# Pacing woven stages by an account of three engines and their buffers

## The chip, the cores and the metric

The kernel runs on one core of one Trainium2 chip. The metric is the time of one execution on the device in microseconds (us); a lower time is better. Before the change the median of the first three runs was 7,900.34 us (7,895.84 to 7,903.62).

The engines are called by their names or as the profile has them: VectorE (DVE), ScalarE (ACT), TensorE (PE; PEld is its weight load), GpSimd (POOL), and SyncE (SP), which starts the transfers (1,321 in the built program; three more are started by ScalarE).

## The reference, cut to what matters

Sixteen images of 32 channels, 128 x 128, pass through four layers. Each layer normalises its input in groups of channels and adds its own result to the input.

```python
x = x + L0(gn(x))   # a row LSTM
x = x + L1(gn(x))   # quantise, then out[f] = -sum over 32 channels and 9 taps of |patch - w[f]|
x = x + L2(gn(x))   # Hartley transform to 32 x 32 modes, mix the channels, transform back
x = x + L3(gn(x))   # five edge operators, normalised; conv1 160 -> 32; a small encoder and decoder
return x
```

Layer 1 fixes the shape of the program. A sum of absolute differences is no matrix product: the differences have to be made elementwise, and only their sum over channels is a product with a matrix of ones.

## The kernel before

Layer 0 fills the first 935 us. Then comes a loop over 16 images x 2 halves x 72 taps, 2,304 in all. One tap makes one tile of 128 x 8,192 differences, on VectorE (`d_dve`, three buffers) or on ScalarE (`d_act`, two buffers), and 16 matmuls on TensorE sum it into four tiles of 128 x 512 in PSUM (called banks here), where the matmuls of this kernel put their results. Taking a result out of PSUM is called an eviction here. A tile's buffer comes free when its sum is done: of the 512 us that VectorE idles before its taps, 476 end with a sum, and 878 of 931 on ScalarE. Between the taps, groups of four images of layers 2 and 3 are woven in as a Python generator. It emits instructions and yields what they cost: a positive number is TensorE time, a negative one is time to wait before going on. The class `Weave` decides after each tap how far the generator may go. The order in which Python emits instructions is the order in each engine's queue, because `keep_order` pins it. The trace of this kernel, set beside the built program by line and tile, keeps to it: ScalarE starts all of its 3,126 instructions in that order, VectorE all but 16 of 7,177, and no matmul starts more than 0.85 us ahead of one that stands before it. So everything below is about the order in which queues are filled; no arithmetic depends on it.

```python
class Weave:
    def advance(self, pe):
        us = (self.dve + self.act) / 2 - self.now      # one clock, the mean of two engines
        self.now += us
        self.credit = min(self.credit + us - pe, 4.0)   # TensorE time that is left over
        self.hold = max(self.hold - us, 0.0)
        self.due(self.now)                              # run the steps put off until now
        if self.credit < 1.0:
            return
        while self.credit > 0 and not self.hold and self.step():
            pass

DVE_US, ACT_US, PE_US = 2.28, 7.1, 0.87

class Differences:
    def run(self, tc, ctx, weave):
        ...
        for i in range(72):
            if i == 3:
                ...                      # new banks, the linear part, the sums of taps 0 to 2
            ...
            act = weave.act + ACT_US < weave.dve + DVE_US and 3 <= i < 68 and len(late) < 2
            t = dp.tile([128, R, P], F16, name="d_act" if act else "d_dve", bufs=2 if act else 3)
            ...
            if act:
                nc.scalar.activation(dst, src, AF.Relu, bias=self.neg[:, i : i + 1])
                weave.act += ACT_US
                late.append((acc, t, i))
            else:
                nc.vector.tensor_scalar(dst, src, self.qw[:, i : i + 1], 0.0, ALU.subtract, ALU.max)
                weave.dve += DVE_US
                while late and (i - late[0][2] > 4 or i == 71):
                    self.sums(*late.pop(0))          # a ScalarE tile: more than 4 taps later
                ...
                self.sums(acc, t, i)                 # a VectorE tile: at once
            weave.advance(4.0 * PE_US + 4.0 if i == 3 else PE_US)
```

What is not yet emitted when the last tap is done (the end of the third group of images and the whole fourth) is emitted by `drain`, and that is the tail of the program.

Of the kernel before, what the change touches and what calls it, by code (L numbers as in the profile page):

```python
# [292 lines left out]
class Weave:  # L293
# [7 lines left out]

    def __init__(self, work):
        self.work, self.pending = work, None
        self.now = self.base = self.credit = self.hold = self.dve = self.act = 0.0
        self.finished, self.count, self.put_off = -1, 0, []
# [6 lines left out]

    def done(self, v):

        if v in self.put_off:
            self.put_off.remove(v)
            v[2]()

    def due(self, now):

        while self.put_off and min(self.put_off)[0] <= now:
            v = min(self.put_off)
            self.put_off.remove(v)
            self.base = v[0]
            v[2]()
        self.base = self.now

    def step(self):

        v = self.pending or next(self.work, None)  # L330
        self.pending = None
        if v is None:
            return False
        if isinstance(v, tuple):
            if v[1] > self.finished:
                self.pending = v
                return False
        elif v < 0:
            self.hold = -v
        else:  # L340
            self.credit -= v
            self.spent = v
        return True

    def advance(self, pe):


        us = (self.dve + self.act) / 2 - self.now
        self.now += us
        self.credit = min(self.credit + us - pe, 4.0)  # L350
        self.hold = max(self.hold - us, 0.0)
        self.due(self.now)
        if self.credit < 1.0:
            return
        while self.credit > 0 and not self.hold and self.step():
            pass


def drain(*weaves):

    live = list(weaves)
    while live:
        w = min(live, key=lambda w: w.now)
        w.spent = 0.0
        go = w.step()
        w.now += w.spent + w.hold
        w.hold = 0.0
        w.due(w.now if go else float("inf"))
        if not go:
# [18 lines left out]
DVE_US, ACT_US, PE_US = 2.28, 7.1, 0.87  # L388


def rest(nc, tc, cst, sel16, bias, m1, r1, a, d, out):


    with ExitStack() as ctx:
# [15 lines left out]
        end.weave.now, end.weave.finished = weave.now, B - 1  # L410
# [3 lines left out]
class Differences:  # L414
# [100 lines left out]
    def finish(self, b, half, acc, xr):  # L515
# [12 lines left out]
        self.weave.later(6.0, store)  # L528
        self.weave.dve += 5.6

    def sums(self, acc, d, i):
        c = 1 if i % 3 == 1 else 0
        for k in range(4):
            for j in range(4):
# [6 lines left out]
                    stop=i == 71,  # L541
# [18 lines left out]
    def run(self, tc, ctx, weave):  # L560
# [12 lines left out]
        before, following = None, self.loaded(0, 0)  # L573
        for b in range(B):
            for half in range(2):
                q = following
                late, ahead, xq = [], [], {}
                for i in range(72):
                    if i == 3:
# [3 lines left out]
                        weave.advance(0.0)  # L583
                        acc = [ps.tile([128, 512], F32, name="acc1") for _ in range(4)]
                        self.linear(acc, q)
                        for t, n in ahead:
                            self.sums(acc, t, n)
# [4 lines left out]
                    if half == 0 and b + 1 < B:  # L592
# [6 lines left out]
                        k = (i - 22) // 15  # L599
                        if 0 <= k < 4 and (i - 22) % 15 == 0:  # L600
# [3 lines left out]
                    act = weave.act + ACT_US < weave.dve + DVE_US and 3 <= i < 68 and len(late) < 2  # L604
# [3 lines left out]
                    dst = t if kw == 1 else t[:, :, :W]  # L608
                    if act:
                        nc.scalar.activation(dst, src, AF.Relu, bias=self.neg[:, i : i + 1])  # L610
                        weave.act += ACT_US
                        late.append((acc, t, i))
                    else:
                        nc.vector.tensor_scalar(dst, src, self.qw[:, i : i + 1], 0.0, ALU.subtract, ALU.max)  # L614
                        weave.dve += DVE_US
                        while late and (i - late[0][2] > 4 or i == 71):
                            self.sums(*late.pop(0))
                        if i < 3:
                            ahead.append((t, i))
                            weave.advance(0.0)  # L620
                            continue
                        self.sums(acc, t, i)
                    weave.advance(4.0 * PE_US + 4.0 if i == 3 else PE_US)
# [5 lines left out]
def normalised(nc, pool, ps, weave, mv, n, avg, eps, out):  # L629
# [6 lines left out]
    yield -4.5  # L636
# [8 lines left out]
    yield -4.5  # L645
# [1171 lines left out]
```

## Time and profile before

| stretch of the profiled execution | us | idle of VectorE | idle of ScalarE |
|---|---|---|---|
| front: layer 0 | 934.7 | | |
| woven: taps of layer 1 with layers 2 and 3 between | 5,707.2 | 913 | 991 |
| tail: what layers 2 and 3 have left | 1,242.8 | | |
| span | 7,884.7 | | |

Idle is the length of the stretch less the engine's busy time in it. The prediction shows the profile's lines for these numbers. A line of waits names who waited for whom, then the total in us, the number of waits and the longest one.

```profile
PE acc L536 <- DVE d_dve L614: 838.8, 567, 28.6
PE acc L536 <- ACT d_act L610: 494.7, 211, 16.4
```

TensorE stands 839 us for VectorE tiles and 495 us for ScalarE tiles.

### The profile page before, as it was taken

What the parts mean: (1) busy time and instruction counts of PE and PEld (TensorE: products, weight loads), DVE (VectorE), ACT (ScalarE), POOL (GpSimd) and SP (SyncE); (2) the same over time, 40 slices, a digit from 0 to 9 for tenths busy, and PEclk for the clock granted to TensorE, in tenths of its full rate; (3) what the DMA queues carried; (4) which work ended last, traced back from release to release, by engine and by line L of the source; (5) the groups of instructions that cost most, each with busy time, mean ns of one, the idle gap of its engine ahead of it and who ended that gap; (6) DMA issues with size and microseconds to landing.
All of it is one profiled execution on the core that took longest, in us unless ns stands there. A gap on an engine that the chain in (4) does not pass through costs nothing. (4 is left out here: it accounts for less than half of the span.)

```text
span 7884.7 us, 258419 instructions
## 1 busy us (share of the span) xinstructions
PE 5635.8 (71%) x121132; PEld 3165.4 (40%) x121132; DVE 5847.9 (74%) x7177; ACT 5406.7 (69%) x3129; POOL 21.6 (0%) x15
## 2 busy tenths in 40 slices
PE   3788366566677668886676666897667765997797
PEld 3665222222253334442343343343335333555564
DVE  7787599989969797887877978888787877134213
ACT  2565488799869879887778877887887885123122
POOL 0000000000000000000000000000000000000000
PEclk9899788888878779998868788998787887897896
DMA  8653111111132431112332432120333233434314
GB/s 319 223 181 130 59 50 60 48 52 39 50 116 80 123 102 51 58 33 67 79 98 90 129 89 73 40 70 34 88 86 101 87 102 94 116 107 122 91 33 90
DMA packets 374269, 721.68 MB, mean 92 GB/s; under 512 B 50896, under 2 KB 219856, under 8 KB 362320
## 3 DMA queue, kind: packets, MB, share of 16 engines
q1 hardware_dynamic: 372768, 704.58, 29.4%
q8 instruction: 949, 15.55, 0.8%
q14 instruction: 120, 0.98, 0.0%
q10 hardware_dynamic: 432, 0.57, 0.0%
HBM read 507.21 MB, written 164.32 MB: 85 GB/s over the span
## 5 line engine op out<-in xcount | busy, mean ns | idle before, releaser
L610 ACT ACTIVATE d_act<-q,neg 128x8192 f16<-128x8192 f16 (+1 forms) x612 | 4332.5, 7137 | 930.9 <-PE acc L536 877.6
L614 DVE TENSOR_SCALAR d_dve<-q,qw 128x8192 f16<-128x8192 f16 (+1 forms) x1692 | 3906.2, 2361 | 512.0 <-PE acc L536 476.3
L536 PE MATMUL acc<-d_dve,sel 128*32 128x512 f16 x27072 | 2007.5, 432 | 861.6 <-DVE d_dve L614 838.8
L536 PEld LDWEIGHTS <-sel 128*32 128x32 f16 x36864 | 1121.1, 106 | 2800.6 <-issue 2196.8
L536 PE MATMUL acc<-d_act,sel 128*32 128x512 f16 x9792 | 784.5, 446 | 499.1 <-ACT d_act L610 494.7
L1519 PE MATMUL acc<-xp,wf 32*32 32x512 f32 x25600 | 986.0, 625 | 29.0 <-issue 16.1
L1519 PEld LDWEIGHTS acc<-xp,wf 32*32 32x32 f32 x25600 | 478.8, 105 | 378.1 <-issue 244.6
L1458 ACT ACTIVATE y<-pooled,b 32x128 f32<-32x128 f32 x512 | 204.6, 400 | 532.2 <-DVE pooled L1444 525.1
L223 PE MATMUL pg<-h,wb 64*64 64x20 f32 (+15 forms) x4096 | 401.2, 323 | 102.4 <-DVE h L255 67.0
L753 PE MATMUL acc<-y,u_conv 32*32 32x256 f32 (+1 forms) x9728 | 402.2, 511 | 79.3 <-issue 35.8
L223 PE MATMUL pg<-e,wb 64*64 64x20 f32 (+15 forms) x4096 | 353.2, 318 | 24.7 <-DVE e L258 10.0
L243 ACT ACTIVATE gt<-pg,bias 128x20 f32<-128x20 f32 (+15 forms) x1024 | 302.7, 377 | 84.2 <-PE pg L223 80.0
L1204 PE MATMUL acc<-xp 32*64 32x204 f32 (+3 forms) x8576 | 247.3, 368 | 130.0 <-ACT xp L1170 107.8
L552 PE MATMUL acc<-q,sel 32*32 32x512 f16 x4608 | 158.6, 556 | 204.9 <-DVE xr L519 115.1
L223 PEld LDWEIGHTS pg<-h,wb 64*64 64x64 f32 x4096 | 243.7, 156 | 140.5 <-DVE h L255 97.6
L223 PEld LDWEIGHTS pg<-e,wb 64*64 64x64 f32 x4096 | 250.6, 158 | 108.3 <-DVE e L258 77.9
L223 PE MATMUL pg<-xn,wb 64*64 64x8 f32 (+60 forms) x4096 | 267.9, 304 | 25.3 <-ACT gt L243 17.4
L1616 ACT ACTIVATE xr<-xr,l_ms 128x1024 f32<-128x1024 f32 x64 | 70.4, 1141 | 305.6 <-DVE xr L1611 254.3
L753 PEld LDWEIGHTS acc<-y,u_conv 32*32 32x32 f32 x9728 | 189.7, 119 | 220.0 <-issue 126.5
L1164 ACT ACTIVATE xp<-xp,fr_shift,stats 128x1280 f32<-128x1280 f32 (+1 forms) x128 | 181.7, 1431 | 136.1 <-DMA xp<-x_d 73.9
L1204 PEld LDWEIGHTS acc<-xp 32*64 32x64 f32 (+1 forms) x8576 | 199.3, 147 | 187.8 <-ACT xp L1170 118.0
L254 ACT ACTIVATE th<-c 128x20 f32<-128x20 f32 (+15 forms) x256 | 81.9, 320 | 222.2 <-DVE c L252 221.2
(203 smaller groups left out, 4247.9 us busy)
## 6 DMA issues: line engine op xcount, KB each, us to landing
xr<-x_d SPq DMA_DIRECT2D x192, 512.0 KB
xp<-x_d SPq DMA_DIRECT2D x112, 640.0 KB
q<-q_d SPq DMA_DIRECT2D x32, 2145.0 KB
x_d<-xr SPq DMA_DIRECT2D x128, 512.0 KB
x_in<-in_x_dram SPq DMA_DIRECT2D x16, 2048.0 KB
res<-in_x_dram SPq DMA_DIRECT2D x64, 512.0 KB
xn<-in_xs_dram SPq DMA_DIRECT2D x64, 512.0 KB
xn<-xn SPq DMA_DIRECT2D x128, 256.0 KB
```

Of the source, the lines that this page charges most:

```text
L223: nc.tensor.matmul(place[q][64 * pair : 64 * pair + 64, :, :width], wb[half, 4 * kind + KIND[q]].rearrange("p b o -> p (b o)"), v[half], s ...
L243: nc.scalar.activation(gt[:, q, :, :n], place[q][:, :, :n], AF.Tanh if q == G else AF.Sigmoid, bias=bias[:, KIND[q] : KIND[q] + 1],)
L254: nc.scalar.activation(th[:, :, :n], cell, AF.Tanh)
L536: self.nc.tensor.matmul(acc[k][32 * j : 32 * j + 32, :], self.sel16[:, i // 9, :], d[:, row : row + 4, c : c + W], start=False, stop=i == 71,)
L552: self.nc.tensor.matmul(acc[k][32 * j : 32 * j + 32, :], self.sel16[rows, 8, :], q[rows, row : row + 4, kw : kw + W], start=tap == 0, stop ...
L610: nc.scalar.activation(dst, src, AF.Relu, bias=self.neg[:, i : i + 1])
L614: nc.vector.tensor_scalar(dst, src, self.qw[:, i : i + 1], 0.0, ALU.subtract, ALU.max)
L753: nc.tensor.matmul(acc[blk][32 * j : 32 * j + 32, o : o + rows * n], t[part, 4 * par + tap, :], src[part, top : top + rows, left : left + ...
L1164: nc.scalar.activation(v, v, AF.Identity, bias=shift[0], scale=self.stats3[:, 1])
L1204: nc.tensor.matmul(gram[blk][j : j + width, at : at + n], xp[part, l, 2 + j : 2 + j + width], xp[part, rows, j : j + width + 4], start=sta ...
L1458: nc.scalar.activation(d, s, AF.Identity, bias=bj)
L1519: nc.tensor.matmul(acc[blk][32 * j : 32 * j + 32, :], tap_of("all", tap)[rows], xp[rows, 4 * j + kh : 4 * j + kh + 4, kw : kw + W], start= ...
```

## The change

The intent: give the emission order a better model. In place of one mean clock, `Weave` keeps a time for each of VectorE, ScalarE and TensorE, lets woven work go as long as TensorE would still be back when the next tap's tile is due, and the loop over the taps also keeps account of when each buffer comes free. Its parts, in the numbering of the prediction's steps where it has one:

- **TensorE's account**: `advance(due)` in place of the credit (step 2); evictions wait for the account's end of TensorE (`SUMMED`) in place of a fixed 4.5 us (step 4); a hand-over, that is a normalised piece that the next stage reads, is a step with a known end (step 3).
- **The tap side**: the engine of a tap is chosen by the accounted end with its buffers, and sums are emitted in the order of the accounted ends (step 1). A ScalarE tap may also be the first of a half (step 5).
- Quantising moves from tap 22 to tap 26 (step 3).

The core of the diff, with cuts:

```diff
-    def advance(self, pe):
-        us = (self.dve + self.act) / 2 - self.now
-        self.now += us
-        self.credit = min(self.credit + us - pe, 4.0)
-        self.hold = max(self.hold - us, 0.0)
-        self.due(self.now)
-        if self.credit < 1.0:
-            return
-        while self.credit > 0 and not self.hold and self.step():
-            pass
+    def lag(self):
+        return 4.5 if self.draining else max(self.pe - self.base, 0.0) + 1.0
+
+    def advance(self, due):
+        while True:
+            self.now = max(self.now, self.dve)
+            self.due(self.now)
+            if self.now < self.until:
+                return
+            self.ready = max(self.ready, self.until)
+            start = max(self.pe, self.ready)
+            if start + 1.0 > due + SLACK:
+                return
+            us = self.step()
+            if us is None:
+                return
+            if us:
+                self.pe = start + us * CLOCK
...
-DVE_US, ACT_US, PE_US = 2.28, 7.1, 0.87
+DVE_US, ACT_US, PE_US = 2.36, 7.15, 1.0
+SLACK, CLOCK = 3.0, 1.0
...
+        free, count = {True: [0.0] * 2, False: [0.0] * 3}, {True: 0, False: 0}
...
+                def sums(until, last):
+                    while late and (min(late)[0] <= until or last):
+                        end, n, act, t = min(late)
+                        late.remove((end, n, act, t))
+                        self.sums(acc, t, n, last and not late)
+                        weave.pe = max(weave.pe, end + 0.2) + PE_US
+                        free[act].append(weave.pe)
...
-                        k = (i - 22) // 15
-                        if 0 <= k < 4 and (i - 22) % 15 == 0:
+                        k = (i - 26) // 15
+                        if 0 <= k < 4 and (i - 26) % 15 == 0:
...
-                    act = weave.act + ACT_US < weave.dve + DVE_US and 3 <= i < 68 and len(late) < 2
+                    ends = {
+                        act: max(weave.act if act else weave.dve, free[act][count[act]]) + (ACT_US if act else DVE_US)
+                        for act in (True, False)
+                        if count[act] < len(free[act])
+                    }
+                    act = False not in ends or (True in ends and i < 68 and ends[True] <= ends[False] + 0.5)
...
-                        while late and (i - late[0][2] > 4 or i == 71):
-                            self.sums(*late.pop(0))
...
-                        self.sums(acc, t, i)
-                    weave.advance(4.0 * PE_US + 4.0 if i == 3 else PE_US)
+                        weave.dve = ends[act]
+                    if acc and (not act or i == 71):
+                        sums(weave.dve, i == 71)
+                    weave.advance(min([v[0] for v in late] + [weave.dve + DVE_US]))
...
-        yield -4.5
+        yield SUMMED
...
-            weave.done(ready[ch, 0])
+            yield ("done", ready[ch, 0])
```

## The prediction

> **What bounds the kernel now.** I read the page first, for the shares of the whole span: VectorE (DVE) 74%, TensorE (PE) 71%, ScalarE (ACT) 69%. Three engines near 70% mean either stages with different limits or a stage in which they hold each other up. So I cut the span where the loop over the taps of layer 1 begins and ends (first and last instruction that writes a difference tile, d_dve on VectorE or d_act on ScalarE) and asked for the busy time in the three stretches:
>
> ```profile
> core 0: us, PE busy (x) PEld busy (x) DVE busy (x) ACT busy (x) POOL busy (x), PEclk, DMA share, GB/s
> 0.00:935.00 935.00, 589.13 (x12324) 447.54 (x12340) 674.38 (x2217) 432.28 (x1354) 2.41 (x7) 0.90 0.56 189
> 935.00:6643.00 5708.00, 4039.92 (x80370) 2075.28 (x80342) 4795.09 (x3986) 4716.00 (x1287) 15.61 (x6) 0.84 0.25 75
> 6643.00:7884.00 1241.00, 1006.74 (x28458) 642.53 (x28450) 378.44 (x976) 258.39 (x489) 3.60 (x2) 0.82 0.36 95
> ```
>
> The change leaves the first 935 us alone. In the middle 5,708 us, which I call the woven stretch, VectorE is idle 5708 - 4795 = 913 us and ScalarE 5708 - 4716 = 992 us: the two share the 2,304 taps, so neither is the bound for the whole stretch and both lose about 17%. The last 1,241 us drain what layers 2 and 3 have left over, and TensorE is busy 1007/1241 = 81% of them.
>
> The groups of instructions give the cost of a tap, and what ended the idle time before it:
>
> ```profile
> L610 ACT ACTIVATE d_act<-q,neg 128x8192 f16<-128x8192 f16 (+1 forms) x612 | 4332.5, 7137 | 930.9 <-PE acc L536 877.6
> L614 DVE TENSOR_SCALAR d_dve<-q,qw 128x8192 f16<-128x8192 f16 (+1 forms) x1692 | 3906.2, 2361 | 512.0 <-PE acc L536 476.3
> L536 PE MATMUL acc<-d_dve,sel 128*32 128x512 f16 x27072 | 2007.5, 432 | 861.6 <-DVE d_dve L614 838.8
> ```
>
> Back to back, a tap costs VectorE 3906.2/1692 = 2.309 us and ScalarE 4332.5/612 = 7.079 us. Both wait for the same thing: the sum of an older tile (16 matmuls), which frees its buffer. TensorE in turn waits 839 us for VectorE tiles in other places. That is not a lack of throughput but the order in its queue. The waits of VectorE in the woven stretch, largest first, account for nearly all of its 913 us:
>
> ```profile
> DVE d_dve L614 <- PE acc L536: 476.3, 198, 11.3
> DVE sides L1234 <- ACT xp L1170: 76.8, 9, 20.8
> DVE xm L934 <- PE acc L930: 65.2, 14, 9.3
> DVE qt L493 <- ACT xq L486: 61.0, 14, 15.3
> DVE xw L988 <- DMA xw<-xm_d: 42.9, 7, 20.4
> ```
>
> I sort the list to its end: 476 for buffers; 138 for ScalarE (sides 77, qt 61); 152 for a product that is to be taken out of PSUM (xm 65, l_ms 29, t 24, s 14, and four small ones); 152 for DMA (xw 43, q 35, xr 26, wf 20, xh 16, xm 13). Last, the timeline of TensorE alone, in a stretch of the first transform of layer 2:
>
> ```profile
> 4055.73 4.88 PE L953 MATMUL acc<-cw,xh 128*128 128x32 f32 x22
> 4060.42 1.90 PE L930 MATMUL acc<-cw,t 128*128 128x32 f32 x8
> 4062.13 3.60 PE L953 MATMUL acc<-cw,xh 128*128 128x32 f32 x16
> 4065.66 1.90 PE L536 MATMUL acc<-d_dve,sel 128*32 128x512 f16 x16
> 4067.48 3.62 PE L953 MATMUL acc<-cw,xh 128*128 128x32 f32 x16
> 4070.92 1.90 PE L930 MATMUL acc<-cw,t 128*128 128x32 f32 x8
> 4072.74 1.90 PE L536 MATMUL acc<-d_act,sel 128*32 128x512 f16 x16
> ```
>
> The sum of the ScalarE tile stands behind transform products, and ScalarE starts its next tap only at 4074.76 after 17.59 us of idling. A sum takes 4067.48 - 4065.66 = 1.8 us here; elsewhere 32 matmuls start and end in 1.9 us, so about 0.9 us a tap.
>
> [...]in the lines above no sum overtakes a transform product. [...]The trace agrees with two rates for one tap's sum (0.9 and 1.8 us) and a mean granted clock of 0.84; an account with one time per sum cannot be right for both. [...]the trace shows such bubbles (198 on VectorE, 136 on ScalarE), but it is the late sum, not the number of buffers alone, that makes them.
>
> **The change part by part.** No arithmetic changes; instructions trade places. I compared the order of both built programs.
>
> (1) Split of the taps: 595 on ScalarE in place of 612, 1,709 on VectorE in place of 1,692. VectorE gains 17 x 2.309 = 39 us, ScalarE loses 17 x 7.079 = 120 us.
>
> (2) Fineness: between two sums of taps TensorE had other work in 443 places before, with 54 matmuls on average, and has 797 now, with 30. Places with 48 or more fall from about 242 to about 133, a factor of 0.55. A 16-matmul tap of conv1 costs 1.14 us (96 records, two for each f32 matmul, in 3.42 us), so 64 in a row held a sum up for 4.6 us. This is what should shrink the 476 us: x 0.55 leaves 260 us.
>
> (3) Hand-overs: a chunk's normalisation becomes a step with a known end for which the account waits, and the quantising of a new image moves from tap 22 to tap 26, 10 taps behind its scaling in place of 6. I let 35 of the 138 us stand.
>
> (4) Evictions: the fixed 4.5 us become the account's own end of TensorE plus 1 us. I let half of 152 stand, 75 us, because the two clock rates aren't in the account. DMA: nothing is moved by it, 145 of 152.
>
> (5) Edges of the halves of an image: ScalarE may now take a tap from the start of a half, where it could not before the fourth. Between its last tap of a half and its first of the next lie 15.6 us on average in the trace (31 edges, 484 us). This helps ScalarE, and so only through the split.
>
> (6) The tail: all groups of layers 2 and 3 stand on the same side of the last tap in both orders, but for the end of group 2's edge statistics: 20 products and 20 reductions and six operations on the folded weights move behind it. 20 x (0.587 + 0.591) + about 8 = 32 us leave the woven stretch, and I add 30 us to the tail, since conv1 of group 2 waits for them there.
>
> Sum. VectorE's work in the stretch: 4795 + 39 - 32 = 4,802. Its idle time: 260 + 35 + 75 + 145 = 515. Stretch: 5,317 us, 391 less. ScalarE then works 4716 - 120 - 10 (five normalisations moved) = 4,586 and idles 731 of it, 261 less than before, of which the edges can give most; so the two engines agree. Span: 935 + 5317 + 1241 + 30 = 7,523; the timed median lies 7900.3 - 7884.7 = 15.6 us above the profiled span, which makes 7,539 us. I say 7,540.
>
> **The rivals.** First, TensorE takes over as the bound. For: in the conv1 windows it is busy 158.9 of 174 us (3,236 to 3,410). Against: over the stretch its 4,040 us are 76% of 5,317. If nothing were gained in the six halves of conv1, whose VectorE idle time is 145 us together, I would lose 0.45 x 145 = 65 us: 7,605. Second, the account is wrong where the clock is low: the three halves with the first transform idle 63, 76 and 63 us on VectorE. If these 202 us stay whole and evictions don't improve, it is some 150 us worse: 7,690. Third, work only moves to the tail. The counts of step 6 speak against it; at worst the drain loses 100 us by another interleaving of its two streams, as finished hand-overs now count 2 us there: 7,610. Fourth, it goes better than I say: all waits on engines gone leaves 4802 + 145, and 7,170 us in all. The DMA waits and the mixed clock make that a bound and not a forecast. Fifth, little comes: VectorE's idle time falls only by 150 us[...], and the time is near 7,790. The best halves of the loop now (136 to 143 us, VectorE idle 8 to 12) show that dense running is possible when little is woven in, so I give this little weight.
>
> **Range and chances.** The term that matters is the idle time left on VectorE, 515 us. From 350 (tight account) to 700 (the second rival) gives 7,375 to 7,725. I widen neither side much: 7,370 to 7,730. Faster by over 2% means below 7,742, that is, at least 158 us of 913 saved net: 0.87. Within 2%: 0.11. Slower: 0.02, since the order only has to be no worse than one made from an average.
>
> **What would show it.** Right: 595 and 1,709 taps, VectorE's wait for sums near 260 us and ScalarE's well under 877; the waits of sides and qt nearly gone; the sums' places finer; first stretch and tail of 935 and about 1,270 us; clock in the woven stretch no lower than 0.84. Wrong: the wait of d_dve for sums still above 400 us, or a new large wait of VectorE on TensorE products; a tail above 1,340 us; conv1 halves at their old 163 to 177 us while others shrink (first rival); the transform halves at their old 227 to 240 us (second rival).

## The result, and the profile after

The changed kernel takes 7,597.75 us (median of four runs, 7,593.22 to 7,622.37) against 7,898.16 us for the kernel before. The ratio is 0.9625, with a 95% interval from 0.9603 to 0.9647. Ratios here are the mean time of one kernel's fast runs over that of the other's of the same rounds, so they are not quite the ratio of the medians quoted. Kernels that ran in different rounds are compared here by these ratios.

The busy times of the engines in the three stretches (columns as the header line says):

```profile
core 0: us, PE busy (x) PEld busy (x) DVE busy (x) ACT busy (x) POOL busy (x), PEclk, DMA share, GB/s
0.00:937.00 937.00, 588.70 (x12324) 446.73 (x12324) 674.44 (x2217) 431.75 (x1354) 2.42 (x7) 0.90 0.56 188
937.00:6312.00 5375.00, 3996.07 (x80334) 1929.04 (x80338) 4797.17 (x3929) 4598.89 (x1264) 17.11 (x6) 0.85 0.26 79
6312.00:7591.00 1279.00, 1043.68 (x28494) 670.42 (x28486) 406.88 (x1051) 262.08 (x495) 3.60 (x2) 0.80 0.36 95
```

The woven stretch loses 334 us, the tail gains 38, the front gains 2. VectorE is as busy as before in the woven stretch (4,797 us against 4,795) and its idle time falls from 913 to 578 us. So the change removed waiting, not work. The granted clock of the stretch is 0.85 after 0.84.

The groups of instructions on the page (busy us, mean ns of one, idle us before them and what ended most of it):

```profile
L661 ACT ACTIVATE d_act<-q,neg 128x8192 f16<-128x8192 f16 (+1 forms) x595 | 4214.6, 7145 | 632.8 <-PE acc L568 596.0
L664 DVE TENSOR_SCALAR d_dve<-q,qw 128x8192 f16<-128x8192 f16 (+1 forms) x1709 | 3942.7, 2362 | 352.6 <-PE acc L568 315.1
L568 PE MATMUL acc<-d_dve,sel 128*32 128x512 f16 x27344 | 1971.3, 418 | 663.7 <-DVE d_dve L664 658.7
```

One tap costs the same as before (7,145 and 2,362 ns, before 7,137 and 2,361; the means mix two widths of tile, and on ScalarE the narrow one takes 7,112 ns and the wide one 7,219, before 7,114 and 7,220). The wait for buffers falls from 878 to 596 us on ScalarE and from 476 to 315 us on VectorE. VectorE's waits in the woven stretch:

```profile
DVE d_dve L664 <- PE acc L568: 315.1, 136, 15.2
DVE xm L979 <- PE acc L975: 97.5, 21, 8.5
DVE es_w L1309 <- DMA gm<-in_gram_dram: 41.1, 2, 21.2
DVE d_dve L664 <- DMA q<-q_d: 34.9, 1, 34.9
DVE xw L1033 <- DMA xw<-xm_d: 33.6, 6, 8.2
```

The waits of `sides` and `qt`, 138 us before, are no longer in the list. `xm`, a transform product to be taken out of PSUM, has grown from 65 to 98 us, and the edge statistics wait twice for a table from memory, 41 us in all, which they did not before. Of TensorE's waits in the same stretch, the two that stood above fell together:

```profile
PE acc L568 <- DVE d_dve L664: 658.7, 474, 25.6
PE acc L568 <- ACT d_act L661: 391.1, 217, 8.6
```

Last, the timeline of TensorE in a transform, to be read against the one in the prediction:

```profile
3938.51 1.90 PE L568 MATMUL acc<-d_act,sel 128*32 128x512 f16 x16
3940.19 1.92 PE L568 MATMUL acc<-d_dve,sel 128*32 128x512 f16 x16
3942.04 2.91 PE L998 MATMUL acc<-cw,xh 128*128 128x32 f32 x24
3944.79 1.18 PE L975 MATMUL acc<-cw,t 128*128 128x32 f32 x8
3945.78 1.89 PE L998 MATMUL acc<-cw,xh 128*128 128x32 f32 x8
3947.61 1.90 PE L568 MATMUL acc<-d_act,sel 128*32 128x512 f16 x16
```

There are still 24 + 8 + 8 = 40 records of products (two for each f32 matmul) between two sums, where the stretch shown of before has at least 46 in front of one sum and 24 in front of the next. What differs is the place: the sum of the ScalarE tile stands close to where its tile is done. ScalarE idles 3.57 us before its tap at 3,940.52 and 1.98 before the one at 3,949.62, where the prediction's stretch showed 17.59 us. The stretch is picked, though: a few taps earlier, at 3,920.54, ScalarE idles 15.72 us in the changed kernel too, and over the woven stretch its waits for sums became fewer (79 in place of 136) and not shorter. So this is only a first hint that the predicted mechanism, finer pieces of woven work, was not what had helped.

### The profile page after: what moved, and what is told of

It reads as the page before. It is cut to its first block, busy times and chain, and to the rows that moved or that the text cites. A ratio compares the mean times of both kernels' runs of the same rounds, so it can differ in the third digit from the quotient of the medians.

```text
span 7591.6 us, 258488 instructions
## 1 busy us (share of the span) xinstructions
PE 5628.5 (74%) x121132; PEld 3046.2 (40%) x121132; DVE 5878.5 (77%) x7194; ACT 5292.7 (70%) x3112; POOL 23.1 (0%) x15
## 5 line engine op out<-in xcount | busy, mean ns | idle before, releaser
L661 ACT ACTIVATE d_act<-q,neg 128x8192 f16<-128x8192 f16 (+1 forms) x595 | 4214.6, 7145 | 632.8 <-PE acc L568 596.0
L664 DVE TENSOR_SCALAR d_dve<-q,qw 128x8192 f16<-128x8192 f16 (+1 forms) x1709 | 3942.7, 2362 | 352.6 <-PE acc L568 315.1
L568 PE MATMUL acc<-d_dve,sel 128*32 128x512 f16 x27344 | 1971.3, 418 | 663.7 <-DVE d_dve L664 658.7
L568 PEld LDWEIGHTS <-sel 128*32 128x32 f16 x36864 | 1075.5, 104 | 2497.8 <-issue 1911.2
L568 PE MATMUL acc<-d_act,sel 128*32 128x512 f16 x9520 | 749.0, 441 | 398.0 <-ACT d_act L661 391.1
L1564 PE MATMUL acc<-xp,wf 32*32 32x512 f32 x25600 | 1010.0, 616 | 40.7 <-issue 23.0
L1564 PEld LDWEIGHTS acc<-xp,wf 32*32 32x32 f32 x25600 | 423.4, 104 | 406.8 <-issue 295.9
L798 PE MATMUL acc<-y,u_conv 32*32 32x256 f32 (+1 forms) x9728 | 434.6, 512 | 76.3 <-issue 42.9
L1685 DVE TENSOR_SCALAR s<-acc,l_ms,l_one 128x512 f32<-128x512 f32 x128 | 100.6, 808 | 181.2 <-PE acc L798 181.2
L1600 DVE TENSOR_TENSOR acc<-acc,cut 128x4 f32<-128x4 f32 x256 | 35.2, 164 | 265.8 <-PE acc L1564 263.6
```

Source lines behind the costliest of these rows:

```text
L568: self.nc.tensor.matmul(acc[k][32 * j : 32 * j + 32, :], self.sel16[:, i // 9, :], d[:, row : row + 4, c : c + W], start=False, stop=last,)
L798: nc.tensor.matmul(acc[blk][32 * j : 32 * j + 32, o : o + rows * n], t[part, 4 * par + tap, :], src[part, top : top + rows, left : left + ...
L1564: nc.tensor.matmul(acc[blk][32 * j : 32 * j + 32, :], tap_of("all", tap)[rows], xp[rows, 4 * j + kh : 4 * j + kh + 4, kw : kw + W], start= ...
L1685: nc.vector.tensor_scalar(s.rearrange("p b r w -> p (b r w)"), acc[blk], istd[:, blk : blk + 1], one[:, blk : blk + 1], ALU.mult, ALU.add,)
```

## The experiments

Two explanations of the smaller wait for buffers stood against each other. By the first, the prediction's step 2, woven work goes in smaller pieces, so a sum has less in front of it. By the second, the tap side does it: the engine of a tap and the order of the sums follow the accounted ends, so TensorE seldom arrives at the sum of an unfinished tile. The other runs test single steps of the prediction.

All times are medians in us, all ratios are to the kernel before in the same rounds. "Woven" and "tail" are the stretches of the profiled execution. The last two columns are waits in the woven stretch: VectorE's `d_dve` for sums, and TensorE's for ScalarE tiles. Numbers of matmuls in a stretch are records of the profile, two for each f32 matmul (41,472 of f16 and 39,830 of f32 are built before, and 121,132 recorded); places and their matmuls are counted in the built programs.

| kernel | time | ratio (95%) | woven | tail | `d_dve` for sums | TensorE for `d_act` |
|---|---|---|---|---|---|---|
| before | 7,898 | 1 | 5,707 | 1,243 | 476 | 495 |
| after | 7,598 | 0.9625 (0.9603 to 0.9647) | 5,374 | 1,281 | 315 | 391 |
| coarse | 7,579 | 0.9599 (0.9583 to 0.9615) | 5,336 | 1,307 | 306 | 405 |
| tapside | 7,858 | 0.9946 (0.9929 to 0.9962) | 5,511 | 1,418 | 597 | 756 |
| choice | 7,853 | 0.9969 (0.9959 to 0.9979) | 5,464 | 1,448 | 576 | 838 |
| nofree | 7,725 | 0.9788 (0.9772 to 0.9805) | 5,336 | 1,449 | 469 | 738 |
| taponly | 7,738 | 0.9821 (0.9804 to 0.9837) | 5,726 | 1,071 | 559 | 336 |
| noedge | 7,561 | 0.9573 (0.9556 to 0.9589) | 5,343 | 1,282 | 230 | 356 |
| quant22 | 7,565 | 0.9582 (0.9563 to 0.9602) | 5,324 | 1,315 | 262 | 392 |
| lag45 | 7,644 | 0.9678 (0.9660 to 0.9695) | 5,409 | 1,283 | 324 | 382 |
| transform | 7,632 | 0.9694 (0.9679 to 0.9708) | 5,415 | 1,289 | 382 | 386 |
| nocoarse | 7,520 | 0.9550 (0.9536 to 0.9565) | 5,306 | 1,286 | 258 | 354 |
| ncspread | 7,523 | 0.9528 (0.9509 to 0.9548) | 5,301 | 1,286 | 251 | 329 |
| nc45 | 7,625 | 0.9659 (0.9634 to 0.9683) | 5,447 | 1,218 | 339 | 397 |

The medians of the kernel before were 7,902.35 us beside the runs coarse, tapside, noedge and lag45, 7,877.39 beside choice, taponly, nocoarse and transform, and 7,887.09 beside nofree, quant22, ncspread and nc45. All results agreed with the reference.

### coarse: long pieces of woven work again, everything else kept

```diff
+        need = 3.0
         while True:
             ...
-            if start + 1.0 > due + SLACK:
+            if start + need > due + SLACK:
                 return
             ...
             if us:
+                need = 1.0
                 self.pe = start + us * CLOCK
-SLACK, CLOCK = 3.0, 1.0
+SLACK, CLOCK = 3.5, 1.0
```

> The changed kernel with one thing undone: the woven work is let out in bursts again. A burst starts only when TensorE has 3 us to spare (and the slack is 3.5 us in place of 3.0, so that as much work stays behind the last tap: 14,397 products against 14,245). By count the places with other work between two sums fall from 797 to 468, with 51 products on average in place of 30, and places with 48 or more rise from 133 to 281; the order of the sums, the choice of the engine for a tap and the hand-overs are as in the changed kernel. Theory 1 (long runs of products ahead of a sum were what cost the time): the wait of d_dve for sums goes back above 430 us, ScalarE's above 750, sides waits for ScalarE again by 50 us or more, and the time is about 7,800 us, two thirds of the gain lost. Rival (the account of the taps themselves, that is order of the sums, buffers and ends, made the gain): no more than 7,660 us and the wait of d_dve below 370 us.

In the built program TensorE has other work between two sums in 468 places, with 50.7 matmuls on average, and 281 of them have 48 or more. That is the coarseness of before (443, 54.0 and 242), where the change has 797, 30.0 and 133. The time is 7,579 us, a ratio of 0.9599: nothing of the gain is lost. The waits in the woven stretch:

```profile
DVE d_dve L666 <- PE acc L570: 306.4, 123, 7.5
PE acc L570 <- ACT d_act L663: 405.2, 216, 13.5
```

The wait for buffers stays at 306 us with pieces as long as before, so step 2 of the prediction falls. Only the size of SLACK differs besides, and it is there to let in about as much woven work; no run changes it alone.

### tapside: the old tap side under the new account of TensorE

```diff
-                    while late and (min(late)[0] <= until or last):
-                        end, n, act, t = min(late)
-                        late.remove((end, n, act, t))
+                    for v in sorted(late, key=lambda v: v[1]):
+                        end, n, act, t = v
+                        if act and i - n <= 4 and not last:
+                            continue
+                        late.remove(v)
                         self.sums(acc, t, n, last and not late)
...
-                    ends = {...}   # with buffers
-                    act = False not in ends or (True in ends and i < 68 and ends[True] <= ends[False] + 0.5)
+                    ends = {True: weave.act + ACT_US, False: weave.dve + DVE_US}
+                    act = ends[True] < ends[False] and acc is not None and i < 68 and sum(v[2] for v in late) < 2
...
-                    weave.advance(min([v[0] for v in late] + [weave.dve + DVE_US]))
+                    weave.advance(min([v[0] for v in late if not v[2]] + [weave.dve + DVE_US]))
```

> The changed kernel with the taps' own rules as before (ScalarE takes a tap when its clock is behind, from the fourth tap of a half on, its sum comes a fixed four taps later, a VectorE tile's sum at once, no account of buffers), and the woven work still let out finely (731 places, 31 products on average). By count 618 taps go to ScalarE and 15,687 products are left behind the last tap in place of 14,245, which alone is worth about 1442 x 1279/14245 = 130 us in the tail, 1,279 us long now. Theory 2 (order of sums, buffers and ends made the gain): woven stretch back to 5,600 us or more, time 7,950 or more. Theory 1: woven stretch 5,450 us or less, tail about 1,410 us, time about 7,780 us.

The pieces stay fine (731 places, 30.7 matmuls), and nearly all of the gain is gone: 7,858 us, 0.9946. TensorE's timeline shows what fine pieces are worth then (start, us, engine, line, what; in brackets the idle time before and what ended it):

```profile
1808.35 1.22 PE L568 MATMUL acc<-d_act,sel 128*32 128x512 f16 x16 [2.95 <-ACT d_act L659]
1809.31 4.38 PE L568 MATMUL acc<-d_dve,sel 128*32 128x512 f16 x48
1815.37 1.05 PE L568 MATMUL acc<-d_act,sel 128*32 128x512 f16 x16 [1.68 <-ACT d_act L659]
1816.22 3.10 PE L568 MATMUL acc<-d_dve,sel 128*32 128x512 f16 x48
```

TensorE stands before the sum of a ScalarE tile that isn't done. Meanwhile VectorE fills all three of its buffers, and then 48 matmuls, the sums of three tiles, run in one go. VectorE has no buffer to write to until the first of these sums is done. Here that costs it only 0.20 us, before its tap at 1,811.32; it adds up over 239 such waits. Over the woven stretch:

```profile
DVE d_dve L662 <- PE acc L568: 596.7, 239, 12.1
PE acc L568 <- ACT d_act L659: 755.5, 279, 14.7
```

Both waits are above even those of before (476 and 495). The woven stretch is 137 us longer than the change's and the tail another 137 us. In the woven stretch TensorE did 77,438 matmuls against 80,334: the account found less room for woven work, and what was left had to be done after the last tap. Neither side's forecast was met: the woven stretch, 5,511 us, lies between the 5,450 and the 5,600 that they named. The tail came as forecast from the count of products (1,418 us, 1,410 expected), so about half of the loss is work left over and about half is the woven stretch itself.

### choice: sums in the order of their ends, but the old choice of the engine

```diff
-                    ends = {...}   # with buffers
-                    act = False not in ends or (True in ends and i < 68 and ends[True] <= ends[False] + 0.5)
+                    ends = {True: weave.act + ACT_US, False: weave.dve + DVE_US}
+                    act = ends[True] < ends[False] and acc is not None and i < 68 and sum(v[2] for v in late) < 2
```

> Half of the tap side undone: the engine for a tap is chosen as before (no account of buffers, no ScalarE tap before the accumulators are there), but the sums stand in the order of the tiles' accounted ends, as in the changed kernel. 617 taps on ScalarE; 16,455 products behind the last tap, 2,210 more than in the changed kernel, worth 2210 x 1279/14245 = 198 us of tail (the same reckoning gave 1,410 us of tail for the run with the whole tap side undone, and 1,418 were measured). Set beside that run only the order of the sums differs. If the order of the sums is what matters: TensorE's wait for ScalarE tiles falls from 723 us there to 400 or less, d_dve's wait for sums from 597 to 350 or less, woven stretch 5,330 us or less (there 5,511), time about 7,760 us or less with the longer tail. If the choice of the engine with its account of buffers matters: the waits stay above 650 and 530 us, woven stretch 5,450 or more, time 7,900 or more.

```profile
DVE d_dve L660 <- PE acc L568: 575.6, 193, 22.2
PE acc L568 <- ACT d_act L657: 837.7, 318, 13.4
```

The time is 7,853 us (0.9969), a little under the 7,900 of the side that came nearer. TensorE waits 837.7 us for ScalarE tiles, more than in any other run, and VectorE 575.6 us for buffers. With this choice the accounted ends leave the buffers out: they put a ScalarE tile's end before it can be, since ScalarE first has to wait for a buffer (527.7 us in 56 waits here). Sums in the order of such ends come too early for the ScalarE tiles. So ordering by ends is worth nothing by itself; the ends have to be right.

### nofree: only the buffers taken out of the accounted ends

```diff
-                        act: max(weave.act if act else weave.dve, free[act][count[act]]) + (ACT_US if act else DVE_US)
+                        act: (weave.act if act else weave.dve) + (ACT_US if act else DVE_US)
```

> The changed kernel with one term taken out of its account: a tap's accounted end no longer waits for the sum that frees its buffer (the edges, the half microsecond in favour of ScalarE, the order by ends and the release of the woven work stay). 615 taps on ScalarE; 16,507 products behind the last tap, worth 2262 x 1279/14245 = 203 us of tail. Theory, formed after the runs with the tap side and its choice undone: without the buffers the ends are too early, the sums of ScalarE tiles stand where the tile isn't done[...]. So TensorE's wait for ScalarE tiles goes from 391 to 750 us or more, d_dve's for sums from 315 to 550 or more, time 7,850 us or more. Rival (the term matters little; the other rules of the choice made the difference): waits below 450 and 370 us, time about 7,598 + 203 - 40 = 7,760 us or less.

```profile
DVE d_dve L664 <- PE acc L568: 468.7, 186, 11.6
PE acc L568 <- ACT d_act L661: 738.2, 318, 11.1
```

This one term is worth 1.6% of the time before (0.9788 against 0.9625), about 130 us, and TensorE's wait for ScalarE tiles goes from 391 to 738 us. The time itself lies between what either side expected, so this run alone decides less than was hoped. Its waits lie with the explanation by buffers for TensorE, and less so for VectorE (469 us). The loss also shows in another stretch than expected: the woven stretch is 38 us shorter than the change's and the tail 168 us longer, because TensorE did only 75,786 matmuls in the woven stretch. That leaves 1.8% between this run and choice (0.9788 and 0.9969). They differ in the edges of the halves and in the 0.5 us by which ScalarE is preferred, and no run tells which of the two counts once the buffers are out of the account.

### taponly: the new tap side in the kernel before

```diff
 # kernel before, with the change's ends, free, count and sums(until, last) in the loop
-DVE_US, ACT_US, PE_US = 2.28, 7.1, 0.87
+DVE_US, ACT_US, PE_US = 2.36, 7.15, 0.87
             self.credit -= v
+            self.pe += v
```

> The kernel before with the tap side of the change alone: sums in the order of accounted ends, buffers in the choice of the engine, 2.36 and 7.15 us for a tap. The release of the woven work is the old one by credit from an average clock (438 places with 62 products on average), hand-overs, evictions and quantising as before. 611 taps on ScalarE; only 11,099 products stay behind the last tap, 3,128 fewer than in the kernel before, worth 3128 x 1241/14227 = 273 us of tail. If the tap side is the larger part of the gain (as undoing it says, some 270 of 300 us): d_dve's wait for sums below 400 us, TensorE's for ScalarE tiles below 420, time about 7,640 us. Rival (it needs the new account of TensorE to work, since a free buffer is told from it): waits as in the kernel before (476 and 476), time 7,800 us or more.

Everything else (the credit, the fixed 4.5 us, the immediate hand-overs, quantising at tap 22) is as before. The time is 7,738 us (0.9821), so about half of the gain.

```profile
DVE d_dve L634 <- PE acc L537: 558.6, 203, 18.2
PE acc L537 <- ACT d_act L631: 336.4, 190, 8.3
```

TensorE stands less before ScalarE tiles, 336 us against 495 before, and less than with the whole change (391). But VectorE waits 559 us for buffers, more than before. The credit lets in more woven work (86,610 matmuls in the woven stretch, where the change has 80,334), without regard to when the next tile is due: in 438 places, with 61.7 matmuls on average. The run coarse has places nearly as long (50.7), set by the account, and 306 us of the same wait. Nor is the old release quite the old one: the two clocks whose mean feeds the credit now contain the accounted waits for buffers, so by the code the credit can grow by more. Neither side's forecast was met (7,640 and 7,800 us). The gain of taponly shows as a tail of 1,071 us and not in the woven stretch.

Taken together with tapside, the two halves of the change are 0.5% (the account of TensorE, with quantising at tap 26) and 1.8% (the tap side alone), and 3.75% together. By the waits, each leaves one of two ways in which TensorE comes late to a VectorE tile: with the tap side undone it stands before ScalarE tiles (756 us); with the account undone it does so less (336 us), and the 559 us of VectorE's wait are left for it to be busy with woven work. The second half of this is read from the lists of waits and not tested by itself.

### noedge: no ScalarE tap before the half has its banks

```diff
-                    act = False not in ends or (True in ends and i < 68 and ends[True] <= ends[False] + 0.5)
+                    act = False not in ends or (True in ends and acc is not None and i < 68 and ends[True] <= ends[False] + 0.5)
```

> The changed kernel, but ScalarE may take no tap of a half before the accumulators are there (as before: not among the first three). 582 taps on ScalarE in place of 595, tail of 14,341 products. If the edges of the halves were worth what step 5 hinted: ScalarE's gap at an edge goes from about 12 to 19 us, 31 x 7 = 217 us of ScalarE or 31 taps' worth, shared by both engines about 217 x 0.246 = 53 us more, so 7,650 us. Rival (the edges give nothing since ScalarE's two buffers are only freed by sums that come after the accumulators): 7,600 us within 15.

The mean gap of ScalarE at the 31 edges of halves, taken as the largest gap near each, was 16.1 us before and is 13.3 in the change; here it is 16.2 again. And yet the time is 7,561 us (0.9573 against the change's 0.9625), with a `d_dve` wait of 230 us. The edges gave no gain at all. Both sides had expected more (7,650 us, and 7,600 within 15).

### quant22: quantising back at tap 22

```diff
-                        k = (i - 26) // 15
-                        if 0 <= k < 4 and (i - 26) % 15 == 0:
+                        k = (i - 22) // 15
+                        if 0 <= k < 4 and (i - 22) % 15 == 0:
```

> The changed kernel with the quantising of a new image back at tap 22. If that move is what took the wait of qt for ScalarE away (61 us before, none now): 45 us or more of it come back and the time rises by 0.75 x 50 = 35 us to about 7,635 us. Rival (the new account of ScalarE's time did it, since a tap given to ScalarE is known to be late): below 15 us of wait, 7,600 us within 15.

The wait of `qt` for ScalarE, 61 us before, does not come back: no such line is in the woven stretch. The wait of `sides` is down to one line (of the window from 935 to 6,700 us, a little longer than the woven stretch):

```profile
DVE sides L1279 <- ACT xp L1215: 1.3, 2, 1.1
```

The time is 7,565 us, below what either side expected, and the ratio 0.9582 is no worse than the change's. So moving the quantising was not needed under the new tap side. Nor was it needed in taponly, where `qt` doesn't wait either. It may be enough by itself: tapside, with the old tap side and tap 26, has no `qt` wait in the woven stretch.

### lag45: evictions after a fixed 4.5 us again

```diff
-        return 4.5 if self.draining else max(self.pe - self.base, 0.0) + 1.0
+        return 4.5
```

> The changed kernel, but results are taken out of PSUM a fixed 4.5 us after they were issued, as before, in place of TensorE's accounted end plus 1 us. Theory 3 (evictions on time matter): VectorE's waits for products other than sums (xm, t, l_ms, s), 106 us now, go to 180 us or more, and the time rises by 0.75 x 75 = 55 us to about 7,655 us. Rival (fineness alone brought them down, or 4.5 us is as good): waits within 20 us of 106 and 7,600 us within 15.

The time is 7,644 us (0.9678 against 0.9625), so longer, but not through the wait that step 4 named. `xm` waits 68.8 us for its product, less than the change's 97.5. What grew is `xw`, for the transfer of `xm` through memory: 68.9 us in place of 33.6. VectorE's wait for sums is 324 us. The run says that the moment of evictions counts; by which wait, it says otherwise than expected.

### transform: the first transform's costs as the trace has them

```diff
-                    return 0.6
+                    return 0.6 if weave.draining else 1.9
...
-                            yield 0.7
+                            yield 0.7 if weave.draining else 0.9
...
-SLACK, CLOCK = 3.0, 1.0
+SLACK, CLOCK = 3.5, 1.0
```

> The changed kernel with two figures of the account set to what its trace shows in the first transform of layer 2: 0.9 us in place of 0.7 for four products with xh, and 1.9 in place of 0.6 for the second product (slack 3.5 in place of 3.0, so that as much stays behind the last tap: 14,421 products). My fourth step let 75 us of waits for products stand and 106 stood, 98 of them before xm. If it is the account's figures that are wrong there[...]: the wait of xm falls below 40 us, VectorE's idle time in each of the three transform halves (59, 56, 59 us) below 40, and the time is some 40 us lower, 7,560 us. Rival (VectorE's wait is the chain product, eviction, DMA itself, which no figure shortens): xm's wait stays above 80 us or comes back at another instruction, and 7,600 us within 15.

This run tests the second rival, an account that is wrong where the clock is low: the change's granted clock is 0.71 in each of the three halves with the transform, and 0.50 from 3,938.5 to 3,942.0 us, where a sum takes 1.90 us. Three waits of VectorE in the woven stretch:

```profile
DVE d_dve L664 <- PE acc L568: 381.9, 148, 18.9
DVE xw L1033 <- DMA xw<-xm_d: 59.9, 15, 7.2
DVE xm L979 <- PE acc L975: 26.9, 8, 6.5
```

The wait of `sides`, gone in the change, is back with 30.2 us in three waits. The costs were wrong indeed: with better ones the wait of `xm` falls from 98 to 27 us, and the three halves with the transform take 211, 207 and 211 us in place of 225, 222 and 225. But the halves behind them take 156, 158 and 156 us in place of 142, 142 and 142, the transfer of `xm` is waited for longer, and so are buffers. The ratio is 0.9694, which is 0.7% worse than the change. The three halves still idle 46, 42 and 46 us on VectorE, where below 40 was expected. The time that the mended wait gave back was taken by others. SLACK went from 3.0 to 3.5 as well, so the 0.7% can't be put down to the two costs alone; coarse has the same SLACK and no loss.

### nocoarse, ncspread, nc45: towards a better kernel

nocoarse is noedge and coarse together. ncspread adds traced costs for the steps that spread a result over an encoder's input. nc45 is nocoarse with more slack.

```diff
 # ncspread: nocoarse, and
-                weave.dve += 0.3
+                weave.dve += 0.5 if wide else 0.28
...
-                weave.act += 0.45
+                weave.act += 0.77 if wide else 0.41
 # nc45: nocoarse, and
-SLACK, CLOCK = 3.5, 1.0
+SLACK, CLOCK = 4.5, 1.0
```

> Two edits that each made the changed kernel no slower, together: no ScalarE tap before the accumulators of a half are there, and the woven work let out in bursts of 3 us. If they act on different waits, the gains add: 7598 - 37 - 19 = 7,540 us, d_dve's wait for sums near 220 us. If both only shift the phase of the same waits: 7,560 us or more.

> The version with no ScalarE tap before the accumulators and with bursts of 3 us (7,520 us), and the account's figures for the spreading of results set to what the traces show: 0.77 us for a 32x512 piece on ScalarE in place of 0.45, 0.50 for a 32x256 piece on VectorE in place of 0.30, and 0.41 and 0.28 for the small ones. In the stage of the small layers a full eviction is 16 x 0.32 = 5 us longer than accounted. If the sums there stand too early for that reason (d_dve waits 64 to 66 us in each of two stretches of 400 us in the changed kernel): 20 to 40 us faster, near 7,490 us. Rival: those waits have other causes, 7,520 us within 15.

> The same version (7,520 us) with slack 4.5 us in place of 3.5: TensorE may run up to 1 us later behind the taps, and 13,099 products stay behind the last tap in place of 14,405, worth 1306 x 1279/14245 = 117 us less of tail. If the woven stretch can take that work for less than TensorE needs for it alone in the tail: woven stretch up by 60 us or less, time about 7,460 us. Rival (three buffers on VectorE hide no more than the 3.5 us): d_dve's wait for sums up from 258 to 400 us, woven stretch up by 117 or more, 7,520 us or more.

nocoarse takes 7,520 us (0.9550), below the 7,540 expected of gains that add, and ncspread 7,523 us (0.9528). They ran in different rounds and their intervals overlap, so the spread costs add nothing that these runs can show. By the ratios both are 0.8 to 1.0% better than the change, which makes them the best versions found. nc45 takes 7,625 us (0.9659): more woven work goes between the taps (82,569 matmuls) and the tail loses 69 us, but the woven stretch grows by 141.

## Why the prediction was right or wrong

**The total and its stretches** were right. The predicted time was 7,540 us, inside a range from 7,370 to 7,730, and 7,597.75 was measured. Part of that is luck, since the largest term, step 2, was reckoned from a mechanism that did not make the gain. The 58 us between them are the woven stretch (5,374 measured, 5,317 predicted: 57 too few), the tail (1,281 against 1,271) and the front (2 more), less 9 us, since the timed median lies only 6 us above the profiled span where 15.6 were assumed (and the sum had been rounded up by 1).

**Step 1, the split**, was right: 595 and 1,709 taps ran, and VectorE's work in the woven stretch was 4,797 us where 4,802 were worked out. ScalarE's was 4,599 against 4,586, its idle time 775 against 731.

**Step 2, the fineness**, was wrong in its mechanism, though its number came near: 315 us were left of 476 where 260 were predicted. The step said that the factor 0.55 in places of 48 or more matmuls "is what should shrink the 476 us". The run coarse puts the long pieces back and keeps 306 us and the whole gain, so fineness was not needed; tapside keeps the pieces fine and loses nearly all of the gain, so it was not enough. That 315 came so near to 260 is luck. In its place stand two things that give together more than the sum of each alone: the tap side, with ends that know the buffers (tapside 0.9946, choice 0.9969, nofree 0.9788 without it), and the account of TensorE (taponly 0.9821 without it). The step confused how long the other work is with where it stands. A long run of products need cost nothing where no tile is due: coarse has 281 places of 48 or more, and 306 us of waiting where the change has 315. The step's ground, that a sum stays behind the products emitted before it, can't be seen from the prediction's lines alone, since they don't show the emitted order. The built programs beside the traces of before and after bear it out: no sum starts ahead of a product of the transform that the lines show. Over all matmul records none starts more than 1.01 us ahead of one that the program has before it, and a sum at most 0.16 us ahead of another product.

**Step 3, the hand-overs**, was right that the waits of `sides` and `qt` would nearly go (138 us to nothing of note, 35 predicted), and wrong about what would do it. Quantising at tap 22 brings nothing back. A build of the changed kernel in which a hand-over doesn't wait for its end differs in 280 of 123,532 places of TensorE's order, in 4 of VectorE's and in none of ScalarE's, so that wait hardly acts; it was not run. What remains for `sides` is the release of woven steps by due time: with the new `advance`, nine runs (the change among them) have at most 2 us of this wait in the woven stretch, and taponly, with the credit, has 27 us. But ncspread has 3.4 us, nc45 10.6 and transform 30.2, so the release doesn't keep it away by itself. No run isolates the cause; it stays open.

**Step 4, evictions and transfers**, was mis-sized: the products to be taken out of PSUM still cost about 106 us of waiting, not 75, and the largest of them, `xm`, grew. Transfers cost about 150 us where 145 were assumed, though not the same ones, with 41 us new for the table of the edge statistics. The reason given, two clock rates in one account (before, 16 matmuls of sums take 1.8 us at 4,065.66 us, where the granted clock is 0.50, and 32 take 1.92 us at 3,008.17, where it is 1.00), is supported by the run transform only as far as the `xm` wait goes. Mending it did not pay.

**Step 5, the edges**, had the gap shrink and so make up most of ScalarE's gain. It shrank from 16.1 to 13.3 us, which is under 90 us over 31 edges, and noedge shows that the time is no worse without it.

**Step 6, the tail**, was right in its number: 38 us more, with 30 predicted. The way to it is less sure: conv1 of group 2 starts 155 us after the last tap's tile where it started after 50, with transform products in front of it, and TensorE is busy 1,044 us in place of 1,007 with about as many matmuls, at a clock of 0.80 in place of 0.82. VectorE's work in the woven stretch agrees, since 4,795 + 39 for the new split would be 4,834 without the 32 us of edge statistics that left it, and 4,797 were measured.

**The rivals.** TensorE did not take over in conv1: those six halves now take 157 to 161 us in place of 163 to 189 (the prediction's 177 leaves out the longest of them), with 77 us of VectorE idle time together in place of 145. Three of them, from 2,985.3 to 3,463.8 us, have TensorE busy 462 of 478.5 us at a mean granted clock of 0.97. The second rival holds half: the halves with the first transform stay at 222 to 225 us (227 to 240 before), with 174 us of idle time of the 202, but the rest of the stretch paid for it. TensorE is busy 170 to 175 us of each of them at a mean granted clock of 0.71; no run here tells whether the small products or the idle time makes the difference from the 0.97. The third, work moved to the tail, came to 38 us. The fourth and the fifth, a far larger gain and a very small one, did not come. That one wait can give way to another is what two runs show on a small scale: in lag45 `xm` fell from 97.5 to 68.8 us and `xw` rose from 33.6 to 68.9, and in transform `xm` fell to 26.9 us and `d_dve` for sums rose from 315 to 382.

**What stays open.** The ratios of noedge, quant22 and coarse came out 0.3 to 0.5% below the change's, those of lag45 and transform 0.5 to 0.7% above. Edits of several kinds, two of them meant to do harm, moved the time by this much in either direction, and the waits that moved were mostly not the ones that the edits were aimed at. The argument here rests on the differences above 1%. Open are also what separates choice from nofree (1.8%), and the part of `advance` that ended the wait of `sides`. One rival is untested: the granted clock of the woven stretch is 0.84 before and in tapside, choice and nofree, and 0.85 or 0.86 in all others. Whether the better order raised it or the clock gave a part of the gain, no run tells; taponly, with 0.85 and little gain, speaks against the clock as the whole.

## What to carry to other kernels

When engines share a few buffers and each starts its work in the emitted order (here to within 1.01 us on TensorE), look first at what the consumer waits for. Here a consumer that stood before unfinished tiles of one producer starved the other producer too: with the buffers left out of the account, TensorE's wait for ScalarE tiles went from 391 to 738 us and VectorE's wait for buffers from 315 to 469 us. An emission order made from accounted ends lost 1.6 of its 3.75% here when the ends left out the wait for a buffer. It gave most when the rest of the consumer's queue was paced by the same account: each half alone gave 0.5% and 1.8%, both 3.75%. And test the mechanism, not only the number: the predicted wait fell about as predicted, for a reason that one run refuted.
